# A tuned attention-and-FFN kernel: loads moved to the head of each round's queue, stores and read-backs behind them, rounding moved into the FFN's first steps

## The chip, the core and the metric

The kernel runs on one core of a Trainium2 chip. The metric is the device time of one execution in microseconds. Before the change three runs took 468.0, 469.41 and 469.4 us; the median is 469.4 us. The profiled execution is a fourth run.

## The reference

The input x has 4 sequences of 512 tokens with 512 features, in float32. The block is an attention-like mixer and then a feed-forward network (FFN), each with a layer norm ahead and a residual around it:

```python
q  = fft(heads(layernorm(x) @ W_q.T))       # 16 heads of 32
kv = fft(heads(layernorm(x) @ W_kv.T))
q, kv = q / norm(q), kv / norm(kv)          # over each head's spectrum
v = ifft(q * cumsum(kv, over tokens)).real
x = x + v @ W_o.T
gate = silu((layernorm(x) @ fp8(gate_w)) * gate_scale)   # 512 -> 1536
up   = (layernorm(x) @ fp8(up_w)) * up_scale
x = x + ((gate * up) @ fp8(down_w)) * down_scale         # 1536 -> 512
```

`fp8(w)` rounds a float32 weight to the nearest float8_e4m3fn value and keeps it as float32. The kernel does this rounding itself.

## The kernel before, in words

**Set-up.** The Fourier matrix is folded into W_q and W_kv, and its inverse into W_o, so that a spectrum is one matrix product. The layer norm's division is left to a per-token factor.

**Rounds.** The tokens are cut into 16 chunks of 128 (N = 16; four chunks to a sequence). One round handles one chunk i, but its steps are spread over several rounds. The program is scheduled by hand: the order of the calls is the order of the instructions on each engine, and the engines wait for each other's semaphores. In round i:

- PE computes the key spectrum of chunk i (`spectrum(i, 1)`, line 368, pq<-wkv), a small transpose (line 356), the query spectrum (`spectrum(i, 0)`, pq<-wq), the running sum of chunk i-1 (line 423, cum<-kh and kl) and the output projection of chunk i-3 (line 467, po).
- DVE scales keys and queries of chunk i-1 (line 392, kn and qn), adds the projection to x (`finish(i - 4)`, line 475), subtracts the rounded part of kn (line 414, kl), transposes the read-back of chunk i-3 (`v_turn`, line 330, qvT<-zv), sums squares (line 384), centres xT of chunk i+1 (`x_center`, line 360) and forms the products of chunk i-1 (lines 440 and 441).
- ACT squares (line 379), rounds kn to kh (line 409), takes the mean of x of chunk i+2 (`x_mean`, line 291) and the deviation of chunk i+1 (line 299).
- POOL computes inverse square roots (lines 301 for the deviations, 389 for the norms rn) and combines the products into qv (`combined`, lines 449 and 450).
- SP's queue issues the transfers in program order: the chunk's two loads for round i+2 (`load_xT`, line 105; `load_x`, line 110), the store of the attention's result (`finish`, line 476, y_all), the raw FFN weights (`load_unit`, line 206, rawf), and for the first sequence the load of ys from y_all (`load_y`, line 485). It also stores qv (`v_out`, line 453) and reads it back in blocks (`v_back`, line 325, four transfers, zv). A transfer that has to wait holds up all that stand behind it in the queue.

In rounds 9 to 12 the statistics of ys (`y_stats`) are computed for the first sequence's FFN; their last step, dev_f, is one POOL instruction (line 301).

**Rounding of the FFN weights.** The weights are cut into 18 units of 128 x 1024. A unit goes through a list of parts on DVE: for a gate or up unit add, (first step of the next unit), sub (lines 248, 229 or 233, 256); for a down unit floor, add, (first step), sub (lines 243, 250, 229 or 233, 258). The list has 60 parts. `next_parts(n)` takes the next n of them; after an add it puts the next unit's absolute value on ACT (`quant_abs`: one instruction at line 218 for a down unit, three at lines 221 to 223 for the others), and outside the rounds a down unit's first step also puts one instruction on POOL (line 239; in the rounds it is ACT's, line 237). Parts use two sets of work buffers, so the absolute value of unit u waits for the sub of unit u-2. The array `given` says how many parts a round takes; a round's parts stand at three places in it.

**FFN.** For each of 4 sequences there are 12 steps (n = 0 to 47 in all). A step is 16 products into gate and up (`inner`, line 539, gu), Silu on ACT (line 550, g), the product with up on DVE (line 552, f), rounding (ACT line 556, fh) and the rest (DVE line 558, fl); then 8 products with the down weights for the step before (`down`, line 573, pd). gate and up have one accumulation bank each, so g of a step must be done before PE starts the next step's gate products, and f before its up products. Parts are taken between f and fl (`between`) and behind the step (`behind`); in step 0 only behind. The last chunks' projections and stores lie in steps 0 to 4, as hooks `on_pe` and `behind`.

**Buffers.** Seven buffers of 8 KB per partition (pool `big`) hold the raw and folded weights, raw FFN units (two units share one), ys, yh and yl.

Of the kernel before, what the change touches and what calls it, by code (L numbers as in the profile page):

```python
# [35 lines left out]
def tile_fft_attention_then_fp8_ffn(  # L36
# [44 lines left out]
    TC = S // P  # L81
# [1 line left out]

    ctx.enter_context(tc.manual_schedule())
    const = ctx.enter_context(tc.tile_pool(name="const", bufs=1))
    big = ctx.enter_context(tc.tile_pool(name="big", bufs=7))
    work = ctx.enter_context(tc.tile_pool(name="work", bufs=2))
    ps = ctx.enter_context(tc.tile_pool(name="ps", bufs=2, space=PSUM))
    dram = ctx.enter_context(tc.tile_pool(name="dram", bufs=1, space=bass.MemoryType.DRAM))
# [4 lines left out]
    N = len(chunks)  # L94
# [18 lines left out]
    def big_tile(name, dtype=F32):  # L113
        return big.tile([P, KC, D], dtype, tag="big", name=name)
# [68 lines left out]
    U1 = 12  # L183
# [14 lines left out]
    def load_unit(u):  # L198

        _, src, n, k = units[u]  # L200
        staged[u] = big_tile("rawf") if k == 0 else staged[u - 1]
        if src is down_w:
            rows = src[n * KC * P : (n + 1) * KC * P, :]
        else:
            rows = src[:, n * D : (n + 1) * D]
        nc.sync.dma_start(
            staged[u][:, k : k + QH, :],
            rows.rearrange("(k p) n -> p k n", p=P)[:, k : k + QH, :],
        )

    def quant_abs(u):
        _, src, _, k = units[u]
        w = staged[u][:, k : k + QH, :]
        a = work.tile([P, QH, D], F32, tag="qa", name=f"qa_{u}")
        m = work.tile([P, QH, D], F32, tag="qm", name=f"qm_{u}")
        c = None
        if src is down_w:
            nc.scalar.activation(a, w, AF.Abs, scale=DOWN)
        else:
            c = work.tile([P, 1], F32, tag="qc", name=f"qc_{u}")  # L220
            nc.scalar.activation(a, w, AF.Abs, scale=UP)
            nc.scalar.activation(m, a, AF.Relu, scale=FAR, bias=far, accum_out=c)
            nc.scalar.activation(c, c, AF.Identity, scale=HUGE, bias=least)
        quant[u] = (w, a, m, c)
# [48 lines left out]
    def next_parts(n, in_rounds=False):  # L273

        for f, u in parts[:n]:
            if f is quant_step:
                f(u, in_rounds)
                if in_rounds and u + 2 < U1 and u != 1:
                    wanted.append(u + 2)
            else:  # L280
                f(u)
            if f is quant_add and u + 1 < len(units):
                quant_abs(u + 1)
        del parts[:n]
# [19 lines left out]
    def stats(src, name):  # L304
        less = mean(src, name)
        return less, deviation(src, less, name)
# [13 lines left out]
    def blocks(z, there):  # L320


        src = there.rearrange("(i t) (k j f) -> j t k i f", t=HD, j=P // HD, f=HD)
        for j in range(P // HD):
            nc.sync.dma_start(
                z[j * HD : (j + 1) * HD].rearrange("t k (i f) -> t k i f", f=HD), src[j]
            )

    def turned(t, z):
        nc.vector.transpose(t.rearrange("p k n -> p (k n)"), z.rearrange("p k n -> p (k n)"))  # L330
# [9 lines left out]
    def nm(i):  # L340
        return "%d_%d" % chunks[i]
# [20 lines left out]
    def spectrum(i, j):  # L362
        if j == 1:
            pqs[i] = {}
        pq = ps.tile([P, D], F32, tag="acc", name=f"pq{j}_{nm(i)}", bufs=4)
        w = (wq, wkv)[j]
        for k in range(KC):
            nc.tensor.matmul(  # L368
                pq, lhsT=xTs[i][:, k, :], rhs=w[:, k, :], start=k == 0, stop=k == KC - 1
            )  # L370
        pqs[i][j] = pq
# [9 lines left out]
    def summed(i, j):  # L381
        sq = sss[i, j]
        ss = work.tile([P, H], F32, tag=f"ss{j}", name=f"ss{j}_{nm(i)}")
        nc.vector.tensor_reduce(ss, heads(sq), AX.X, ALU.add)  # L384
        sss[i, j] = ss
# [15 lines left out]
    def k_scaled(i):  # L401
        kn = work.tile([P, D], F32, tag="kn", name=f"kn_{nm(i)}", bufs=1)
        scaled(i, 1, kn)
        if i in carries:
            row = carries.pop(i)
            nc.vector.tensor_tensor(kn[:1, :], kn[:1, :], row, ALU.add)
        kh = work.tile([P, D], F32R, tag="kh", name=f"kh_{nm(i)}", bufs=3)
        kl = work.tile([P, D], F32R, tag="kl", name=f"kl_{nm(i)}", bufs=3)
        nc.scalar.copy(kh, kn)
        kns[i] = (kn, kh, kl)  # L410
# [41 lines left out]
    def v_out(i):  # L452
        nc.sync.dma_start(qv_all[i], qvs.pop(i)[0])

    def v_back(i):
        zs[i] = work.tile([P, KC, P], F32, tag="z", name=f"zv_{nm(i)}")
        blocks(zs[i], qv_all[i])

    def v_turn(i):
        qvTs[i] = work.tile([P, KC, P], F32, tag="qvT", name=f"qvT_{nm(i)}", bufs=1)  # L460
        turned(qvTs[i], zs.pop(i))

    def project(i, tag="b"):
        po = ps.tile([P, D], F32, tag=tag, name=f"po_{nm(i)}")
        qvT = qvTs.pop(i)
        for k in range(KC):
            nc.tensor.matmul(  # L467
                po, lhsT=qvT[:, k, :], rhs=wo[:, k, :], start=k == 0, stop=k == KC - 1
            )
        pos[i] = po  # L470
# [10 lines left out]
    def load_y(b, chunks=None):  # L481
        if b not in ys:
            ys[b] = big_tile(f"ys_{b}")
        for c in range(TC) if chunks is None else chunks:
            nc.sync.dma_start(ys[b][:, c, :], y_all[b, c])

    def y_stats(b, c):
        st_y[b, c] = stats(ys[b][:, c, :], f"f{b}_{c}")
# [100 lines left out]
    def pair(n):  # L589

        return range(2 * n, 2 * n + 2) if 0 <= n < TC // 2 else ()

    def at(f, i, *more):
        if 0 <= i < N:
            f(i, *more)
# [83 lines left out]
    products(1)  # L679
    combined(1)  # L680
    v_back(0)
    v_out(1)
    summed(2, 0)
    norms(2, 0)
    next_parts(2, True)


    given = [2 if i in (6, 8, 10) else 3 for i in range(N - 3)] + [2, 2, 0]
    for i in range(3, N):
        spectrum(i, 1)  # L690
        at(load_xT, i + 2)
        k_scaled(i - 1)
        at(finish, i - 4)
        at(load_x, i + 2)
        while wanted:
            load_unit(wanted.pop(0))
        if 0 <= i - (N - 9) < TC:
            load_y(0, [i - (N - 9)])
        v_back(i - 2)
        k_low(i - 1)  # L700
        v_turn(i - 3)
        at(x_row, i + 1)
        squared(i, 1)
        at(x_deviation, i + 1)
        next_parts(given[i] // 3, True)
        q_scaled(i - 1)
        summed(i, 1)
        norms(i, 1)
        spectrum(i, 0)
        next_parts((given[i] + 1) // 3, True)  # L710
        running(i - 1)
        squared(i, 0)
        carry(i - 1)
        at(x_mean, i + 2)
        if 0 <= i - (N - 7) < TC:
            y_stats(0, i - (N - 7))
        at(x_center, i + 1)
        products(i - 1)
        combined(i - 1)
        v_out(i - 1)  # L720
        if i == N - 1:
            y_transpose(0, TC - 2)
            y_transpose(0, TC - 1)
        summed(i, 0)
        norms(i, 0)
        for c in pair(i - (N - 3)):
            y_norm(0, c)
        next_parts((given[i] + 2) // 3, True)
        project(i - 3)
        if i == N - 2:  # L730
            y_transpose(0, 0)
            y_transpose(0, 1)

    v_back(N - 2)
    load_unit(U1)
    load_unit(U1 + 1)
    load_y(1)
    finish(N - 4)  # L740
    k_scaled(N - 1)
# [4 lines left out]
    def on_pe(n, part):  # L746
        if part == 1 and n == 0:
            running(N - 1)
            products(N - 1)
            combined(N - 1)  # L750
            v_out(N - 1)
            project(N - 3, "tp")
            v_back(N - 1)

    def on_act(n):
# [3 lines left out]

    def between(n):  # L760
        if 0 < n < MC:
            next_parts(1)

    def behind(n):
        b, m = divmod(n, MC)
        if n == 1:
            load_unit(U1 + 2)
            load_unit(U1 + 3)
            finish(N - 3)
            v_turn(N - 2)  # L770
        elif n == 2:
            project(N - 2, "tp")
            v_turn(N - 1)
        elif n == 3:
            finish(N - 2)
            project(N - 1, "tp")
            load_unit(U1 + 4)
            load_unit(U1 + 5)
        elif n == 4:
            finish(N - 1)  # L780
        if b + 1 < B:
            if m == 0 and b > 0:
                load_y(b + 1)
            if 0 <= m - 7 < TC:
                y_turn(b + 1, m - 7)
            if 0 <= m - 4 < TC:
                y_norm(b + 1, m - 4)
                y_blocks(b + 1, m - 4)
        if b == 0:
            next_parts(2)  # L790
        if b + 1 < B and 0 <= m - 3 < TC:
            y_deviation(b + 1, m - 3)
# [77 lines left out]
```

## Time and profile before

| | us |
|---|---|
| median of the runs | 469.4 |
| profiled execution | 470.05 |
| its span, first to last instruction | 468.3 |
| set-up and rounds 0 to 2 (to the start of round 3) | 40.5 |
| rounds 3 to 15 (to the first FFN product) | 149.8 |
| FFN and the last stores | 278.0 |

The granted clock of TensorE was 0.997 of full speed. In the profile's timelines a row gives the start in us from the span's start, the duration, the engine, the line, the operation, what it writes and reads, and in brackets how long the engine had been idle and what ended that wait. SPq is SP's queue: its rows are the issues of transfers, not their data.

### The profile page before, as it was taken

The page shows a single profiled execution, that of the slowest core. Times are in us where ns is not written, and L with a number is a line of the kernel's source. Part 1 is how long each engine was busy: PE and PEld are TensorE (multiplying, and loading weights), DVE is VectorE, ACT ScalarE, POOL GpSimd, SP SyncE. Part 2 cuts the span into 40 slices and gives each one's busy share as a digit, 9 for nine tenths or more (in the row PEclk, how much of TensorE's full clock was granted, in tenths as well). Part 3 has the DMA queues.
Part 4 walks back from the last instruction along what each step waited for, and adds up shares of the span by engine and source line. Part 5 has one row for each costly group of instructions (what it writes and reads, how often), then busy time and mean ns, then how long its engine had stood idle before and what let it go on. Part 6 is the DMA issues. An engine that isn't in the chain of part 4 may idle for free.

```text
span 468.3 us, 5038 instructions
## 1 busy us (share of the span) xinstructions
PE 454.3 (97%) x1672; PEld 307.9 (66%) x1672; DVE 281.2 (60%) x387; ACT 213.2 (46%) x429; POOL 189.5 (40%) x133
## 2 busy tenths in 40 slices
PE   6999999999999989999999999999999999999995
PEld 6544344444444435676888888888888888888883
DVE  1549898998789789886797353333433332522325
ACT  3663664655576553255763225533236433222220
POOL 0248887899778677620043140112210022400002
PEclk9999999999999999999999999999999999999998
DMA  8733466657554632374442050340040430200002
GB/s 280 282 112 90 115 189 177 184 169 208 156 146 121 176 78 65 69 235 142 149 98 45 0 172 9 83 97 0 23 158 24 96 61 1 90 1 0 0 1 90
DMA packets 82586, 49.13 MB, mean 105 GB/s; under 512 B 62080, under 2 KB 62464, under 8 KB 82560
## 3 DMA queue, kind: packets, MB, share of 16 engines
q1 hardware_dynamic: 82176, 48.79, 36.9%
q8 instruction: 13, 0.21, 0.2%
q14 instruction: 13, 0.11, 0.1%
q10 hardware_dynamic: 384, 0.03, 0.1%
HBM read 33.04 MB, written 15.73 MB: 104 GB/s over the span
## 4 chain that ended last, share of the span: by engine, by line
PE 66%; POOL 14%; DVE 9%; issue 5%; ACT 4%; DMA 1%; SPq 0%; ACTq 0%; DVEq 0%; POOLq 0%
PE gu L539 37%; PE pd L573 19%; POOL rn L389 10%; PE po L467 4%; PE pq L368 3%; POOL qv L449 2%; POOL qv L450 1%; DVE ss L384 1%; PE pkv L164 1%; ACT sq L379 1%; DVE wu L256 1%; DVE qv L440 1%; PE pw L179 1%; DVE cross L441 1%; DVE kn L392 1%
## 5 line engine op out<-in xcount | busy, mean ns | idle before, releaser
L389 POOL TENSOR_TENSOR rn<-ss,nhalf 128x16 f32<-128x16 f32 x32 | 105.5, 3297 | 14.1 <-DVE ss L384 14.1
L552 DVE SCALAR_TENSOR_TENSOR f<-gu,gus,g 128x512 f32<-128x512 f32 x48 | 36.0, 750 | 110.8 <-PE gu L539 109.0
L539 PE MATMUL gu<-yh,wg 128*128 128x512 f32 x192 | 76.4, 398 | 0.0
L573 PE MATMUL pd<-wd,fl 128*128 128x512 f32 x192 | 74.8, 390 | 0.0
L573 PE MATMUL pd<-wd,fh 128*128 128x512 f32 x192 | 74.8, 389 | 0.0
L539 PE MATMUL gu<-yh,wu 128*128 128x512 f32 x192 | 74.8, 389 | 0.0
L539 PE MATMUL gu<-yl,wg 128*128 128x512 f32 x192 | 74.8, 389 | 0.0
L539 PE MATMUL gu<-yl,wu 128*128 128x512 f32 x192 | 74.7, 389 | 0.0
L556 ACT CAST fh<-f 128x512 fp32r<-128x512 f32 x48 | 29.8, 621 | 80.6 <-DVE f L552 80.6
L368 PE MATMUL pq<-wkv,xT 128*128 128x512 f32 x128 | 58.3, 598 | 2.4 <-DVE xT L360 2.4
L550 ACT ACTIVATE g<-gu,gus 128x512 f32<-128x512 f32 x48 | 33.0, 687 | 59.9 <-PE gu L539 59.6
L467 PE MATMUL po<-wo,qvT 128*128 128x512 f32 x128 | 57.9, 595 | 0.4
L368 PE MATMUL pq<-wq,xT 128*128 128x512 f32 x128 | 57.6, 593 | 0.0
L558 DVE TENSOR_TENSOR fl<-f,fh 128x512 fp32r<-128x512 f32 x48 | 35.8, 745 | 27.6 <-ACT fh L556 27.5
L585 POOL TENSOR_TENSOR o<-o,ys 128x512 f32<-128x512 f32 x14 | 17.7, 1290 | 81.7 <-DVE o L583 72.7
L368 PEld LDWEIGHTS pq<-wkv,xT 128*128 128x128 f32 x128 | 23.7, 190 | 33.4 <-issue 25.3
L301 POOL TENSOR_TENSOR dev_f<-dev_f,nhalf 128x1 f32<-128x1 f32 x16 | 10.1, 629 | 88.0 <-ACT dev_f L300 86.3
L539 PEld LDWEIGHTS gu<-yl,wg 128*128 128x128 f32 x192 | 36.1, 188 | 8.3 <-issue 1.0
L368 PEld LDWEIGHTS pq<-wq,xT 128*128 128x128 f32 x128 | 23.2, 190 | 27.8 <-issue 26.9
L539 PEld LDWEIGHTS gu<-yh,wg 128*128 128x128 f32 x192 | 36.0, 188 | 8.3 <-issue 0.5
L573 PEld LDWEIGHTS pd<-wd,fl 128*128 128x128 f32 x192 | 36.1, 188 | 7.6 <-DVE fl L558 0.2
L539 PEld LDWEIGHTS gu<-yh,wu 128*128 128x128 f32 x192 | 36.0, 188 | 7.5
(89 smaller groups left out, 607.3 us busy)
## 6 DMA issues: line engine op xcount, KB each, us to landing
x<-in_x SPq DMA_DIRECT2D x16, 256.0 KB, 4.1
xT<-in_xT SPq DMA_DIRECT2D x16, 256.0 KB, 2.9
qv_all<-qv SPq DMA_DIRECT2D x16, 256.0 KB, 2.0
zv<-qv_all SPq DMA_DIRECT2D x64, 64.0 KB, 4.1
y_all<-x SPq DMA_DIRECT2D x16, 256.0 KB, 3.0
ys<-y_all SPq DMA_DIRECT2D x16, 256.0 KB, 4.2
out<-o SPq DMA_DIRECT2D x16, 256.0 KB, 2.1
rawf<-in_gate_w SPq DMA_DIRECT2D x6, 512.0 KB, 5.0
```

The source lines that it names most:

```text
L301: nc.gpsimd.tensor_tensor(rstd, rstd, nhalf[:, 0:1], ALU.pow)
L368: nc.tensor.matmul(pq, lhsT=xTs[i][:, k, :], rhs=w[:, k, :], start=k == 0, stop=k == KC - 1)
L389: nc.gpsimd.tensor_tensor(rns[i, j], sss.pop((i, j)), nhalf, ALU.pow)
L449: on.tensor_tensor(vh[:, :, 1:HK], vh[:, :, 1:HK], vh[:, :, HK + 1 :], ALU.subtract)
L467: nc.tensor.matmul(po, lhsT=qvT[:, k, :], rhs=wo[:, k, :], start=k == 0, stop=k == KC - 1)
L539: nc.tensor.matmul(p, lhsT=w[:, k, m * P : (m + 1) * P], rhs=v[:, k, :], start=k == 0 and v is yhs[b], stop=k == KC - 1 and v is yls[b],)
L550: nc.scalar.activation(g, pgu[0], AF.Silu, scale=gus[:, 0, m : m + 1])
L552: nc.vector.scalar_tensor_tensor(f, pgu[1], gus[:, 1, m : m + 1], g, ALU.mult, ALU.mult)
L556: nc.scalar.copy(fh, f)
L558: nc.vector.tensor_tensor(fl, f, fh.bitcast(F32), ALU.subtract)
L573: nc.tensor.matmul(pds[b][c], lhsT=v[:, c * P : (c + 1) * P], rhs=wd[:, m, :], start=m == 0 and v is fused[n][0], stop=m == MC - 1 and v i ...
L585: add.tensor_tensor(o, o, ys[b][:, c, :], ALU.add)
```

## The change

- The pool `big` has eight buffers, not seven.
- In each round, the two loads for round i+2 and the load of ys go to the head of the queue, ahead of the stores and raw loads.
- `v_out` of a chunk is no longer called at the end of its round but one round later, right ahead of its own `v_back`, behind the loads, the y_all store and the raw loads.
- `y_stats` moves from ahead of `x_center`, `products` and `combined` to behind them.
- `given` is lowered: rounds 11 and 12 take two parts, not three; round 13 one, not two; round 14 none, not two. Steps 1 to 3 of the FFN take three parts, not one, between f and fl.
- At the end of the rounds and in the first FFN steps, raw units 12 and 13 are loaded ahead of the store and read-back of chunk 14, units 14 and 15 ahead of the read-back of chunk 15, and units 16 and 17 in step 1 (before: step 3).

The sum of the work is the same, but for one instruction: in the FFN the first step of unit 10 puts its extra instruction on POOL, where the round's version puts it on ACT. In the built program SP's load of units 14 and 15 waits for DVE and ACT (the last use of units 8 and 9), and that of units 16 and 17 for the last use of units 10 and 11.

```diff
-    big = ctx.enter_context(tc.tile_pool(name="big", bufs=7))
+    big = ctx.enter_context(tc.tile_pool(name="big", bufs=8))
...
     v_back(0)
-    v_out(1)
     summed(2, 0)
...
-    given = [2 if i in (6, 8, 10) else 3 for i in range(N - 3)] + [2, 2, 0]
+    given = [2 if i in (6, 8, 10, 11, 12) else 3 for i in range(N - 3)] + [1, 0, 0]
     for i in range(3, N):
+
+        at(load_xT, i + 2)
+        at(load_x, i + 2)
+        if 0 <= i - (N - 9) < TC:
+            load_y(0, [i - (N - 9)])
         spectrum(i, 1)
-        at(load_xT, i + 2)
         k_scaled(i - 1)
         at(finish, i - 4)
-        at(load_x, i + 2)
         while wanted:
             load_unit(wanted.pop(0))
-        if 0 <= i - (N - 9) < TC:
-            load_y(0, [i - (N - 9)])
+        v_out(i - 2)
         v_back(i - 2)
...
         at(x_mean, i + 2)
-        if 0 <= i - (N - 7) < TC:
-            y_stats(0, i - (N - 7))
         at(x_center, i + 1)
         products(i - 1)
         combined(i - 1)
-        v_out(i - 1)
+        if 0 <= i - (N - 7) < TC:
+            y_stats(0, i - (N - 7))
...
-    v_back(N - 2)
     load_unit(U1)
     load_unit(U1 + 1)
+    v_out(N - 2)
+    v_back(N - 2)
     load_y(1)
...
             v_out(N - 1)
             project(N - 3, "tp")
+            load_unit(U1 + 2)
+            load_unit(U1 + 3)
             v_back(N - 1)
...
         if 0 < n < MC:
-            next_parts(1)
+            next_parts(3 if n < 4 else 1)
...
         if n == 1:
-            load_unit(U1 + 2)
-            load_unit(U1 + 3)
             finish(N - 3)
             v_turn(N - 2)
+            load_unit(U1 + 4)
+            load_unit(U1 + 5)
...
             project(N - 1, "tp")
-            load_unit(U1 + 4)
-            load_unit(U1 + 5)
```

## The prediction

> **What bounds the kernel now.** I read the engine rows of the page first, then the timeline of PE, then those of SP, ACT and POOL around the places where PE starts late.
>
> ```profile
> PE 454.3 (97%) x1672; PEld 307.9 (66%) x1672; DVE 281.2 (60%) x387; ACT 213.2 (46%) x429; POOL 189.5 (40%) x133
> ```
>
> PE is busy for 97% of the span, so only its lost time can be won. Busy time has modelled ends; I therefore count from start to start. Each round i begins with the key spectrum, pq<-wkv. Cut at these starts, rounds 10 to 14 look so (length of the stretch, then the busy time of each engine):
>
> ```profile
> core 0: us, PE busy (x) PEld busy (x) DVE busy (x) ACT busy (x) POOL busy (x), PEclk, DMA share, GB/s
> 118.20:129.10 10.90, 10.90 (x29) 4.81 (x27) 7.73 (x12) 5.27 (x13) 8.00 (x6) 1.00 0.53 166
> 129.10:141.36 12.26, 11.67 (x28) 4.83 (x27) 9.94 (x15) 8.80 (x21) 9.60 (x7) 1.00 0.58 136
> 141.36:152.70 11.34, 11.14 (x28) 4.92 (x28) 10.34 (x15) 7.97 (x19) 9.52 (x7) 1.00 0.45 133
> 152.70:164.31 11.61, 11.15 (x28) 4.92 (x28) 8.49 (x12) 6.62 (x16) 7.94 (x7) 1.00 0.69 172
> 164.31:178.37 14.06, 12.65 (x35) 5.84 (x36) 12.20 (x18) 7.35 (x15) 10.97 (x6) 1.00 0.34 71
> ```
>
> Rounds 6 to 10 start 10.88 to 10.90 us apart, with no idle PE: that is PE's own floor. Rounds 11, 12, 13 are 1.38 + 0.46 + 0.73 longer; in PE's timeline the next spectrum then waits for DVE's centred xT. Round 14 holds eight transposes (0.87), so it loses 2.31; in it the running sum waits 1.06 for kh. Together 4.9 us. Round 15 and the FFN run without a gap (a step is 5.44 us again and again), and round 3, 12.34 us long, loses 1.46. DVE, ACT and POOL keep their order up to round 8, so that one stays. Why rounds 11 to 13 are long is seen in three queues at once.
>
> ```profile
> 135.30 0.33 SPq L453 DMA_DIRECT2D qv_all<-qv  x1
> 135.73 0.38 SPq L105 DMA_DIRECT2D xT<-in_xT  x1
> 136.20 0.40 SPq L476 DMA_DIRECT2D y_all<-x  x1
> 136.65 0.43 SPq L110 DMA_DIRECT2D x<-in_x  x1
> ...
> 146.64 0.33 SPq L453 DMA_DIRECT2D qv_all<-qv  x1
> ```
>
> ```profile
> 141.23 0.63 ACT L291 ACTIVATE each<-x 128x512 f32<-128x512 f32 x1 [2.47 <-DMA x<-in_x]
> ...
> 143.92 0.29 ACT L300 ACTIVATE dev_f<-dev_f,eps 128x1 f32<-128x1 f32 x1
> ```
>
> ```profile
> 144.29 0.55 POOL L301 TENSOR_TENSOR dev_f<-dev_f,nhalf 128x1 f32<-128x1 f32 x1 [0.81 <-ACT dev_f L300]
> 144.81 0.70 POOL L449 TENSOR_TENSOR qv<-qv 128x240 f32<-128x240 f32 x1
> 145.59 1.02 POOL L450 TENSOR_TENSOR qv<-cross 128x240 f32<-128x240 f32 x1
> ```
>
> This is a ring. The store of qv stands ahead of the loads, so x is issued 1.35 us after it and lands 4.58 later; ACT waited 2.47 for it and then needs 2.9 to reach dev_f; POOL takes dev_f ahead of qv; the next qv store follows at 146.64. The ring takes 11.34 us, and 11.75 the next time (146.64 to 158.39): more than PE's 10.88. The lag that it leaves is what makes kh late in round 14.
>
> **Part 1: loads first, store and read-back behind.** xT and x of round i+2 now follow the previous round's read-back, which waits for nothing of this round. The ring is cut: x no longer waits for qv. The cost is at the store. y_all (waits for DVE's x) and, in eight rounds (4, 5, 6, 8, 9, 10, 12, 13), a 512 KB raw load now stand ahead of the qv store, and the read-back stands right behind it and waits for its landing. When the store led the queue it landed in 2.0 us (the page's median). The row that is nearest to the new order is at the end of the rounds:
>
> ```profile
> 196.84 1.08 SPq L206 DMA_DIRECT2D rawf<-in_gate_w  x2
> 198.01 1.95 SPq L485 DMA_DIRECT2D ys<-y_all  x4
> 200.06 0.38 SPq L476 DMA_DIRECT2D y_all<-x  x1
> 200.54 0.40 SPq L453 DMA_DIRECT2D qv_all<-qv  x1
> 207.23 2.60 SPq L325 DMA_DIRECT2D zv<-qv_all  x4
> ```
>
> Here the store stood behind 2.36 MB and its read-back was issued 6.7 us later: 2.6 MB in 10.4 us, 0.25 MB per us. The Trainium skill (DMA: Bandwidth & Descriptors, "Queues, rings and completion order") speaks against the change: the engines consume a queue's descriptors in ring order, and a transfer's semaphore lands only after the earlier writes of that engine. By the 2.0 us row the wait is unchanged; by the rule, at this row's rate, 1.05 MB (y_all, raw, qv) need 4.2 us plus some 2 to land, less 0.95 already gone: 5.2 us. I take 5. Then zv is complete about 0.1 + 0.45 (y_all's issue) + 0.5 (raw's) + 5 + 2.6 (the read-back's four issues) + 2.7 (landing of the last; 2.2 at least, 4.1 in the median) = 11.4 us after DVE's x. In round 4 x ends at 58.03, so zv is there at 69.4, where the turn began at 68.54: DVE waits 0.9. The centred xT would be done at 73.8 instead of 72.9; PE needs it at 74.68. In round 8, with a ys load too, x ends at 100.39, zv comes at some 112.5 where the turn began at 110.19; xT is then done near 117.6, and PE needs it at 118.20. So the cost is nothing, covered by 0.6 us at the tightest place; each us that landing takes beyond that is lost in that round. If landing stays at 2.0, nothing is lost either.
>
> x itself: the read-back ends at most 2.8 us into the next round, xT, x and landing make it 8.2; ACT takes it 8.8 after the round's start at the earliest (round 8: 105.21 - 96.44). Covered; what is late next is zv.
>
> **Part 2: ys statistics behind the combining.** On POOL four dev_f (0.55 each) move behind qv; qv no longer waits for ACT (0.8 to 2.5 us a round). The next norms wait at most for dev_f, which is then done. Nothing is added.
>
> **Part 3: five rounding parts leave rounds 11 to 14 (one, one, one, two).** A part takes DVE 0.6 to 1.2 us from start to start; most are 1.2. DVE was busy 9.94, 10.34, 8.49 and 12.20 us in these rounds; without five parts (some 5.3 us) and with the ring cut, the heaviest has about 10 of its 11.75. POOL is busy 8 to 11 us with its 3.3 us norms, so it has no more than one us of room in a round. I let 0.7 us of the 4.9 stay: **4.2 us won**.
>
> **Part 4: these parts in the FFN.** DVE takes them between f and fl and behind the step. Steps 1, 2, 3 hold five parts instead of three. In the built program's order on DVE, with start-to-start costs f 0.67, fl 0.60, x and turn 0.6 each, L256 1.20, L243 1.14, L250 1.11, L258 1.13, L248 1.16, L229 and L233 0.60, in the times of before:
> - Step 1: f at 201.78, three parts 3.45, fl from 205.9 to 206.5; PE wants it at 206.97. Then x, turn, two parts: the next f starts at 209.5 instead of 207.25.
> - Step 2: its third part waits for ACT's three-instruction abs chain (2.57 us); fl ends at 214.3, wanted at 215.85. The turn of the last chunk comes at 214.3 instead of 212.41, and is wanted at 217.67. L258 ends at 216.1.
> - Step 3: here ACT counts. The abs chain of unit 13 needs the buffer that this L258 frees, and stands ahead of g on ACT: 216.1 + 2.57, so g runs from 218.7 instead of 214.24; PE needs its bank at 221.1. Unit 14's chain starts at 222.05, ahead of y's deviation (1.04) and the next g, which ends at 226.35; PE needs it at 226.56.
> - Step 5: g ends at 232.0, needed at 232.0. From unit 16 on the chain is one instruction of 1.06, and ACT catches up.
>
> No wait appears if every row keeps its mean; but margins are 0.0 to 0.5 at three places. DVE parts beside POOL's L239 took up to 1.73 (199.39), 0.5 more. POOL has one such operation more, since unit 10's moves from ACT (1.15). I charge **0.6 us**; bounds 0 and 2.
>
> **Part 5: the eighth buffer.** Raw units 8 and 9 now live beyond round 14, where yh and yl need two buffers; that is what it pays for. Loads of units 14, 15 come some 9 us earlier, at 201, ahead of the last read-back: 1.2 us of issue and 1 MB behind the store. That read-back waited to 207.23 before, so it is not later. Loads 16, 17 wait for the last use of units 10, 11 (about 212) and two y_all stores stand behind them on SP; those y rows are read one batch later. Cost nothing; bounds -0.3 and 0.3.
>
> **The sum.** 468.3 - 4.2 + 0.6 = 464.7 us of span. The profiled execution took 470.05, 1.75 around its span, so 466.45 of its own time; the median of the runs, 469.4, is 0.65 below it: **465.8 us**.
>
> **Rivals.**
> - All of the 4.9 comes back and the FFN holds: 464.5. For it: rounds 6 to 10 ran at the floor with up to three parts.
> - The read-back takes the ring's place: landing behind the raw load takes 6.5, not 5, and rounds 7, 9 and two later ones lose 0.5 each: 467.6. For it: 6.7 was seen. Against: with 2.36 MB ahead, not 0.8.
> - The rounds stay bound by POOL's norms and DVE, and the cut ring was only the last of equal waits; 0.7 comes back: 468.9, no change. Against: DVE waits of 2.18 us for POOL begin with dev_f's wait.
> - Slower: in FFN steps 1 to 3 the parts run at 1.7 instead of 1.2 beside POOL: fifteen parts, 7.5 us later, less 1.2 of margin: 6.3 lost through ACT's g behind the abs chain, 469.4 - 4.9 + 6.3 = 470.8 or more. It decides from L258 of step 2 ending after 218. Against: one part of twenty here took as long.
>
> **Chances.** The forecast 0.55, all back 0.13, read-back 0.14, no change 0.10, slower 0.08. About 0.3% (1.4 us) is what a measurement of this kernel can tell from no change. Faster below 468.0: 0.80, with part of the read-back case left to the same, 0.12; slower 0.08. The range reaches from all back with run scatter (463.6) to the no-change case (469.3).
>
> **What would show it.** Right: rounds 11 to 13 start 10.9 apart and round 14 takes 11.8; no ACT wait on x; dev_f behind qv; qv to zv 4 to 6 us in rounds with a raw load; in steps 3 to 5 PE gaps under 0.5 us before gu. Wrong: turns that wait for zv with PE waiting for xT or qvT behind them; gaps before gu or pd of over 1 us in steps 1 to 5; rounds 11 to 13 above 11.3 without an x wait.

## The result and the profile after

The changed kernel takes 465.0 us (median of four runs, 464.31 to 465.4) where the kernel before took 468.9 beside it: a ratio of 0.9917, 95% interval 0.9894 to 0.9941. The profiled execution took 465.4 us, its span 463.6. The prediction said 465.8 for the median and 464.7 for the span.

This is the row of engines on the page of the changed kernel, and then its time cut at the starts of rounds 11 to 15 (columns as in the table by round before):

```profile
PE 452.5 (98%) x1672; PEld 308.5 (67%) x1672; DVE 280.9 (61%) x387; ACT 211.9 (46%) x428; POOL 192.6 (42%) x134
```

```profile
core 0: us, PE busy (x) PEld busy (x) DVE busy (x) ACT busy (x) POOL busy (x), PEclk, DMA share, GB/s
...
129.38:140.25 10.87, 10.87 (x28) 4.99 (x27) 9.41 (x14) 8.79 (x20) 9.86 (x8) 1.00 0.57 143
140.25:151.14 10.89, 10.89 (x29) 5.00 (x28) 9.43 (x14) 8.72 (x21) 9.87 (x6) 1.00 0.58 158
151.14:162.01 10.87, 10.87 (x28) 4.99 (x27) 7.32 (x13) 4.97 (x13) 8.75 (x7) 1.00 0.62 168
162.01:173.77 11.76, 11.76 (x37) 5.82 (x35) 10.00 (x15) 3.80 (x8) 10.26 (x8) 1.00 0.33 77
```

PE is busy without a gap in all four stretches, as in the two rounds before them. Rounds 11, 12 and 13 went from 12.26, 11.34 and 11.61 us to 10.87, 10.89 and 10.87; round 14 went from 14.06 to 11.76, which is the floor and its eight transposes. All of the 4.9 us came back. From the start of round 10 to the FFN's first product (its row starts at 189.86 before and at 185.01 after) it is 71.66 us before and 66.51 after: 5.15 us, since round 15 is 0.25 shorter as well. The FFN and the last stores take 278.39 us before and 278.60 after; the start-up was 0.30 longer in this execution. 5.15 - 0.21 - 0.30 = 4.64, the difference of the two spans before rounding (468.26 and 463.61). (By these starts the last two rows of the table of before are 149.4 and 278.4, not 149.8 and 278.0.)

The medians differ by less, 3.9, because the profiled execution of before was 1.2 above the median of its runs and that of the changed kernel 0.4. There is one trace of before, and its excess lies most likely in the rounds: its round 10 starts at 118.20 (117.6 to 119.0 in the ten other traces that differ only later), and its FFN takes as long as in the other traces with the same FFN (278.4). A median execution of before would then have a stretch of 468.7 - 1.75 - 118.3 - 278.4 = 70.3 us; this is an estimate, from the 1.75 us that the profiled execution took beyond its span and the mean start of these ten. The 5.15 is thus about 3.8 in a median execution. In the later comparisons the executions of before spread from 467.3 to 471.2, those of the changed kernel by 1.1. Of the 15 above 470, nine show a mean granted clock of 0.995 or less, of the other 53 two; where in them the clock fell is not known.

SP's queue in round 10 and after it: the loads stand ahead, and the store of qv stands behind y_all and the raw load.

```profile
120.48 0.43 SPq L110 DMA_DIRECT2D x<-in_x  x1
...
121.48 0.38 SPq L476 DMA_DIRECT2D y_all<-x  x1
121.90 0.43 SPq L206 DMA_DIRECT2D rawf<-in_up_w  x1
122.43 0.43 SPq L453 DMA_DIRECT2D qv_all<-qv  x1
128.22 2.61 SPq L325 DMA_DIRECT2D zv<-qv_all  x4
...
131.59 0.38 SPq L110 DMA_DIRECT2D x<-in_x  x1
132.81 0.33 SPq L476 DMA_DIRECT2D y_all<-x  x1
133.23 0.38 SPq L453 DMA_DIRECT2D qv_all<-qv  x1
136.36 2.61 SPq L325 DMA_DIRECT2D zv<-qv_all  x4
```

The read-back waits for the store's landing: 5.8 us with a raw load ahead of the store, 3.1 without. ACT gets x in time now; it waits for nothing but its own last transfer's issue:

```profile
138.45 0.63 ACT L291 ACTIVATE each<-x 128x512 f32<-128x512 f32 x1 [0.60 <-ACT end L430]
...
141.13 0.29 ACT L300 ACTIVATE dev_f<-dev_f,eps 128x1 f32<-128x1 f32 x1
```

And POOL takes dev_f behind qv; when qv starts (140.19), ACT has not yet computed dev_f (141.13 to 141.42):

```profile
140.19 1.40 POOL L449 TENSOR_TENSOR qv<-qv 128x240 f32<-128x240 f32 x1
141.68 0.70 POOL L450 TENSOR_TENSOR qv<-cross 128x240 f32<-128x240 f32 x1
142.33 1.00 POOL L301 TENSOR_TENSOR dev_f<-dev_f,nhalf 128x1 f32<-128x1 f32 x1
```

### The profile page after: what moved, and what is told of

It reads as the page before. It is cut to its first block, busy times and chain, and to the rows that moved or that the text cites. A ratio compares the mean times of both kernels' runs of the same rounds, so it can differ in the third digit from the quotient of the medians.

```text
span 463.6 us, 5026 instructions
## 1 busy us (share of the span) xinstructions
PE 452.5 (98%) x1672; PEld 308.5 (67%) x1672; DVE 280.9 (61%) x387; ACT 211.9 (46%) x428; POOL 192.6 (42%) x134
## 4 chain that ended last, share of the span: by engine, by line
PE 92%; DVE 3%; ACT 3%; issue 1%; DMA 1%; ACTq 0%; SPq 0%; DVEq 0%
PE gu L539 38%; PE pq L368 19%; PE pd L573 19%; PE po L467 11%; PE cum L423 1%; PE pkv L164 1%; PE pw L179 1%; ACT sq L379 1%; PE pw L164 1%; ACT qm L222 1%; DMA raw<-in_w_kv 1%; ACT each L299 0%; ACT qa L221 0%; PE pt_f L317 0%; DVE ss L384 0%
## 5 line engine op out<-in xcount | busy, mean ns | idle before, releaser
L389 POOL TENSOR_TENSOR rn<-ss,nhalf 128x16 f32<-128x16 f32 x32 | 103.6, 3238 | 16.3 <-DVE ss L384 13.8
L301 POOL TENSOR_TENSOR dev_f<-dev_f,nhalf 128x1 f32<-128x1 f32 x16 | 12.5, 781 | 72.1 <-ACT dev_f L300 72.0
```

The lines of the kernel that those rows point to most:

```text
L301: nc.gpsimd.tensor_tensor(rstd, rstd, nhalf[:, 0:1], ALU.pow)
L389: nc.gpsimd.tensor_tensor(rns[i, j], sss.pop((i, j)), nhalf, ALU.pow)
```

## The experiments

Three things are changed: the queue order (Q), the place of the ys statistics (Y), and the moved parts with the eighth buffer and the earlier raw loads (P). Runs 1 to 6 are all the other combinations of the three. The traces are compared by one number, the stretch from the start of round 10 to the FFN's first product, which leaves out the start-up; the medians and ratios are of runs beside the kernel before (median 468.7 in each of the three groups; 468.9 beside the change itself). The stretch is that of one execution. The one of before was 1.4 above the median of 468.7 and that of run 1 1.3 above its own, all others of the table within 0.5, so differences of the stretch against these two can be off by that much; the medians stand beside them.

| run | kernel | median us | ratio to before, 95% | stretch us | rounds 10 to 14 us |
|---|---|---|---|---|---|
| | before | 468.7 | | 71.66 | 10.90 12.26 11.34 11.61 14.06 |
| 1 | Q | 468.05 | 0.9979 (0.9966 to 0.9993) | 70.13 | 11.40 11.21 11.21 10.98 13.83 |
| 2 | Y | 466.13 | 0.9927 (0.9900 to 0.9953) | 67.55 | 10.89 10.87 10.88 10.88 12.54 |
| 3 | P | 466.88 | 0.9951 (0.9927 to 0.9975) | 68.69 | 10.88 10.96 12.19 10.98 12.43 |
| 4 | Q, Y | 466.26 | 0.9934 (0.9908 to 0.9959) | 67.55 | 10.88 10.88 10.88 10.88 12.54 |
| 5 | Y, P | 465.12 | 0.9921 (0.9900 to 0.9943) | 66.51 | 10.88 10.88 10.88 10.88 11.75 |
| 6 | Q, P | 465.39 | 0.9931 (0.9912 to 0.9951) | 66.90 | 10.88 10.88 10.88 10.88 12.14 |
| | Q, Y, P: the change | 465.0 | 0.9917 (0.9894 to 0.9941) | 66.51 | 10.88 10.87 10.89 10.87 11.76 |

**Run 1, the queue order alone.**

```diff
     for i in range(3, N):
+        at(load_xT, i + 2)
+        at(load_x, i + 2)
+        if 0 <= i - (N - 9) < TC:
+            load_y(0, [i - (N - 9)])
         spectrum(i, 1)
...
+        v_out(i - 2)
         v_back(i - 2)
...
         combined(i - 1)
-        v_out(i - 1)
```

> The kernel before with only the queue order of the change (loads first, store of qv behind y_all and raw load); ys statistics ahead of the combining, rounding parts and buffers as before. Ring theory: the ring is cut at SP, rounds 11 to 13 start 10.9 apart, round 14 (two parts in it) loses up to 1; span some 464.9, median 465.5 to 466 (3 less than before). Rival (the parts on DVE and the POOL work of these rounds are what is late): nothing in them changes, rounds 11 to 14 still lose over 3.5, median 468 to 469.

It won 1.5 us of the stretch and 0.6 of the median: far from the 3 of the ring theory, and inside the rival's range, but not nothing. ACT's waits for x are gone, and yet rounds 11 and 12 take 11.21. POOL shows both reasons: first the wait for the first dev_f (round 9's statistics), then a turn in which it waits only for DVE's sums of squares.

```profile
121.83 0.66 POOL L301 TENSOR_TENSOR dev_f<-dev_f,nhalf 128x1 f32<-128x1 f32 x1 [2.30 <-ACT dev_f L300]
...
139.81 3.89 POOL L389 TENSOR_TENSOR rn<-ss,nhalf 128x16 f32<-128x16 f32 x1 [0.94 <-DVE ss L384]
143.66 1.25 POOL L301 TENSOR_TENSOR dev_f<-dev_f,nhalf 128x1 f32<-128x1 f32 x1
144.89 0.70 POOL L449 TENSOR_TENSOR qv<-qv 128x240 f32<-128x240 f32 x1
145.66 1.03 POOL L450 TENSOR_TENSOR qv<-cross 128x240 f32<-128x240 f32 x1
146.66 2.90 POOL L389 TENSOR_TENSOR rn<-ss,nhalf 128x16 f32<-128x16 f32 x1
...
151.01 3.88 POOL L389 TENSOR_TENSOR rn<-ss,nhalf 128x16 f32<-128x16 f32 x1 [0.93 <-DVE ss L384]
```

```profile
149.59 0.75 DVE L392 SCALAR_TENSOR_TENSOR qn<-pq,dev,rn 128x512 f32<-128x512 f32 x1 [0.89 <-POOL rn L389]
150.26 0.67 DVE L384 TENSOR_REDUCE ss<-sq 128x16 f32<-128x512 f32 x1
```

The second is a loop of two engines: POOL's key norm, dev_f, qv, query norm, then DVE's qn and ss, then POOL's next key norm: 139.81 to 151.01, 11.20 us, with no wait but the hand-overs. Cutting the ring at SP leaves this loop, and dev_f in it. The other runs show which of the two counts.

**Run 2, the ys statistics alone.** The kernel before, with this edit only:

```diff
-        if 0 <= i - (N - 7) < TC:
-            y_stats(0, i - (N - 7))
         at(x_center, i + 1)
         products(i - 1)
         combined(i - 1)
         v_out(i - 1)
+        if 0 <= i - (N - 7) < TC:
+            y_stats(0, i - (N - 7))
```

> The kernel before with only the ys statistics moved behind the combining. Ring theory: the ring is cut at POOL, since qv no longer waits for ACT, but ACT still gets x late; half or more of the 4.9 comes back, span some 465.8, median 466.5. Rival (SP's order or the parts count, dev_f's place does not): median 468 to 469.

This one edit wins 4.1 of the stretch's 5.15 us and 2.5 of the median: rounds 11 to 13 are at the floor, with SP's queue and all parts as before. The POOL rows of the same place as the first of run 1:

```profile
113.76 3.88 POOL L389 TENSOR_TENSOR rn<-ss,nhalf 128x16 f32<-128x16 f32 x1 [0.38 <-DVE ss L384]
117.61 0.70 POOL L449 TENSOR_TENSOR qv<-qv 128x240 f32<-128x240 f32 x1
...
120.09 0.56 POOL L301 TENSOR_TENSOR dev_f<-dev_f,nhalf 128x1 f32<-128x1 f32 x1 [0.56 <-ACT dev_f L300]
```

qv follows its norm at once. dev_f comes at the same time as before (120.08 there): ACT is not earlier, it only no longer holds up qv. The row of before, for comparison:

```profile
120.08 0.55 POOL L301 TENSOR_TENSOR dev_f<-dev_f,nhalf 128x1 f32<-128x1 f32 x1 [2.48 <-ACT dev_f L300]
```

The ring is cut at POOL just as well, because qv no longer waits for anything that x feeds: in rounds 10 to 12 ACT's longest wait for x is 1.04, where it was 3.73. The loop of POOL and DVE is not cut: dev_f stays in it, one place later, and it takes 11.35 us here (key norm at 136.72, the next at 148.07), no less than in run 1. DVE's turns (qn to qn) are 11.48, 11.49 and 11.35, all above 10.88, and PE loses nothing in rounds 10 to 13. So what this edit takes away is the one wait of round 9, and not the loop.

**Run 3, the moved parts alone.** `given`, the FFN's parts, the eighth buffer and the raw loads as in the change; queue and statistics as before.

```diff
-    given = [2 if i in (6, 8, 10) else 3 for i in range(N - 3)] + [2, 2, 0]
+    given = [2 if i in (6, 8, 10, 11, 12) else 3 for i in range(N - 3)] + [1, 0, 0]
...
-            next_parts(1)
+            next_parts(3 if n < 4 else 1)
```

> The kernel before with only the five rounding parts moved into the FFN's first steps, the eighth buffer and the earlier raw loads. Ring theory: the ring stays, rounds 11 to 13 still take 11.3 to 11.7, only round 14 gains; span some 466.5, median 467. Rival (parts are the load that is late): rounds 11 to 13 go to 10.9, all comes back, median 465 or less.

As the ring theory had it in the median (466.88), but not in the shape: the ring did not hold each round at 11.3 to 11.7. DVE's turn from one qn to the next, from round 9 on 13.61, 12.26, 11.34 and 12.20 us before, is 13.10, 12.01, 11.59 and 10.73 here: the lag of round 9 stays, and comes out at PE in round 12 (1.04 of waiting for xT).

**Run 4, the parts undone.** Queue order and statistics, everything else as before.

```diff
-    given = [2 if i in (6, 8, 10, 11, 12) else 3 for i in range(N - 3)] + [1, 0, 0]
+    given = [2 if i in (6, 8, 10) else 3 for i in range(N - 3)] + [2, 2, 0]
...
-            next_parts(3 if n < 4 else 1)
+            next_parts(1)
```

> The changed kernel without the moved parts and the eighth buffer: queue order and ys statistics alone. Ring theory: rounds 11 to 13 start 10.9 apart with their three, three and two parts; round 14 with two parts loses up to 1 through kh; the FFN's 0.2 comes back; median 465 to 466. Rival (parts needed): rounds 11 to 14 lose 2 or more, median 467 or more.

466.26 us, between the two. The stretch is that of run 2 to 0.01 us: on top of the statistics the queue order is worth nothing. The parts are worth 67.55 - 66.51 = 1.04 on top of both: 0.78 in round 14 and 0.25 in round 15. From here the theory was another: what counted is that qv waited for dev_f, and not SP's order.

**Run 5, the queue order undone.** The changed kernel with the loads and `v_out` back in the places of before.

```diff
-        at(load_xT, i + 2)
-        at(load_x, i + 2)
         spectrum(i, 1)
+        at(load_xT, i + 2)
         k_scaled(i - 1)
         at(finish, i - 4)
+        at(load_x, i + 2)
...
-        v_out(i - 2)
         v_back(i - 2)
...
         combined(i - 1)
+        v_out(i - 1)
```

> The changed kernel with its queue order undone (the order of the kernel before: qv store first, loads behind it); ys statistics behind the combining, moved parts and eighth buffer stay. New theory after the first four runs (what counted was that qv on POOL waited for dev_f; SP's order is not on the path): rounds 10 to 13 at 10.88, round 14 at 11.8, median 464.8 to 465.2, as the whole change. The prediction's ring (x late behind the qv store holds ACT and by it the round): ACT waits on x again, rounds 11 to 13 lose 0.3 to 0.7 each, median 466 or more.

465.12 us, where the new theory had it, and the same stretch as the change. ACT does not wait for x at all in rounds 9 to 13, although the loads stand behind the qv store again. The largest part of the diff makes no difference that these runs can tell.

**Run 6, the statistics undone.** The changed kernel with `y_stats` back ahead of `x_center`.

```diff
+        if 0 <= i - (N - 7) < TC:
+            y_stats(0, i - (N - 7))
         at(x_center, i + 1)
         products(i - 1)
         combined(i - 1)
-        if 0 <= i - (N - 7) < TC:
-            y_stats(0, i - (N - 7))
```

> The changed kernel with only the ys statistics put back ahead of the combining; queue order, parts and buffer stay. New theory: in round 9 POOL's qv waits 2.3 to 2.7 for the first dev_f, dev_f stays in the loop of POOL and DVE, whose turn with fewer parts is 10.9 to 11.2; some 1.5 is lost in rounds 10 to 14, median 466 to 466.5. The prediction's ring (cut at SP already): nothing is lost, median 465.

465.39 us, nearer to the prediction's ring than to the new theory. The wait came as foreseen, and DVE's turn took 13.11 there:

```profile
119.97 0.67 POOL L301 TENSOR_TENSOR dev_f<-dev_f,nhalf 128x1 f32<-128x1 f32 x1 [2.45 <-ACT dev_f L300]
```

But the next turns, with fewer parts, took 11.21, 10.61 and 10.74, so the lag shrank again before PE met it, and only 0.39 of the expected 1.5 was lost (in round 14). Queue order and parts without the statistics thus win 4.76 of the 5.15 us, more than the statistics alone. The wait costs PE time only where the later turns keep its lag.

**Run 7, the FFN's extra parts crowded into step 1.**

```diff
         if 0 < n < MC:
-            next_parts(3 if n < 4 else 1)
+            next_parts(6 if n == 1 else 2 if n == 2 else 1)
```

> The changed kernel with the FFN's extra parts crowded: six parts between f and fl in step 1, two in step 2, one in step 3 (instead of three, three, three). Cover theory of part 4 (fl of step 1 has 0.5 us of room): three more parts of 1.1 to 1.2 make fl 3 us late, PE waits 2.5 to 3.3 for it before the down products, median 467.5 to 468.3. Rival (PE finds other work, or the down products come later): under 0.5, median 465.5 or less.

470.21 us, ratio 1.0028 (1.0013 to 1.0042): 5.1 to 5.2 slower than the change, more than the expected 3.3. PE's rows, and then the windows around them:

```profile
202.32 0.39 PE L573 MATMUL pd<-wd,fh 128*128 128x512 f32 x1
206.03 0.50 PE L573 MATMUL pd<-wd,fl 128*128 128x512 f32 x1 [3.32 <-DVE fl L558]
...
208.09 4.93 PE L467 MATMUL po<-wo,qvT 128*128 128x512 f32 x8
```

```profile
core 0: us, PE busy (x) PEld busy (x) DVE busy (x) ACT busy (x) POOL busy (x), PEclk, DMA share, GB/s
...
207.00:208.00 1.00, 1.00 (x4) 0.82 (x4) 1.00 (x2) 0.00 (x0) 0.00 (x0) 0.67 0.55 209
208.00:209.00 1.00, 1.00 (x3) 0.40 (x2) 1.00 (x3) 0.00 (x0) 0.00 (x0) 0.50 0.15 53
209.00:210.00 1.00, 1.00 (x3) 0.48 (x2) 1.00 (x2) 0.40 (x1) 0.00 (x0) 0.50 0.48 57
210.00:211.00 1.00, 1.00 (x2) 0.38 (x2) 1.00 (x2) 0.49 (x2) 0.00 (x0) 0.62 1.06 408
```

fl was late by what the cover theory said, so its 0.5 us of room is real. The rest is the clock: after 3.32 us of idle PE the granted clock falls to 0.50, from 207.3 until about 210.8. The windows' losses, 0.33 + 0.50 + 0.50 + 0.38, are 1.7 us; 3.3 + 1.7 = 5.0. The Trainium skill has this rule (TensorE: Matmul & The Clock Gate, "Why this matters for your kernels": no idle gaps of PE above some 3 us between bursts of products, or the clock falls to half). The expectation had left it out: by the wait alone 468.3, with it 470; 470.21 was measured.

**Run 8, round 3 relieved.** No parts ahead of round 3; three instead of two in rounds 11 and 12.

```diff
     norms(2, 0)
-    next_parts(2, True)
...
-    given = [2 if i in (6, 8, 10, 11, 12) else 3 for i in range(N - 3)] + [1, 0, 0]
+    given = [2 if i in (6, 8, 10) else 3 for i in range(N - 3)] + [1, 0, 0]
```

> The changed kernel without the two rounding parts ahead of round 3, and with three parts instead of two in rounds 11 and 12 (the same parts in the same order, each up to two places later until there). If round 3's 1.47 comes from these parts on DVE ahead of the centred xT: round 3 takes 10.9 to 11.3, median 463.6 to 464. If it comes from DVE's and POOL's own chain at the start: round 3 stays 12.3, and rounds 12 to 14 may lose up to 1 through the parts: 465 to 466.

464.37 us, ratio 0.9909 (0.9890 to 0.9929), a little above the expected 464. Round 3's loss does come from the parts: it takes 11.13 instead of 12.35. These are DVE's rows at its start in the changed kernel, and then in run 8:

```profile
43.43 0.68 DVE L229 TENSOR_SCALAR qm<-qa 128x1024 int32<-128x1024 int32 x1
44.03 1.73 DVE L256 SCALAR_TENSOR_TENSOR wg<-qm,qc,qa 128x1024 fp32r<-128x1024 f32 x1
45.68 0.74 DVE L392 SCALAR_TENSOR_TENSOR kn<-pq,dev,rn 128x512 f32<-128x512 f32 x1
```

```profile
43.64 0.75 DVE L392 SCALAR_TENSOR_TENSOR kn<-pq,dev,rn 128x512 f32<-128x512 f32 x1 [0.46 <-POOL rn L389]
```

Counted from the round's start (40.78 and 40.45), kn came 1.7 us earlier. In round 7, though, another order of parts now falls due, and it takes 11.23; round 8 takes 10.99. Of 1.22 won 0.46 was given back there.

**Runs 9 and 10, which of the four statistics counts.** Both are run 1 (queue order alone) with part of run 2: in run 9 only the first of the four is behind the combining, in run 10 only the other three.

```diff
-        if 0 <= i - (N - 7) < TC:
+        if 0 < i - (N - 7) < TC:
             y_stats(0, i - (N - 7))
         at(x_center, i + 1)
         products(i - 1)
         combined(i - 1)
+        if i == N - 7:
+            y_stats(0, 0)
```

> The kernel of the first run (queue order alone) with only the first of the four ys statistics (round 9) behind the combining; the other three stay ahead of it. Theory of the one wait (ACT cannot give the first dev_f before some 120 us, so qv on POOL waits 2.3 there and the lag is never made up): nearly all of the gain of all four comes back, round 9's turn at qn takes 11.2 to 11.5 instead of 12.94, rounds 10 to 13 at 10.9, median 466 to 466.8. Theory of the loop (dev_f, 1.25 in every turn of POOL and DVE): 467.5 to 468.

> The kernel of the first run (queue order alone) with the first of the four ys statistics (round 9) ahead of the combining and the other three behind it. Theory of the one wait: the lag of 2.3 comes in round 9 as before and stays, median 467.6 to 468.1 as with none moved. Theory of the loop: rounds 10 to 13 go to 10.9 and the lag shrinks, median 466 to 466.8.

Run 9: 466.59 us, ratio 0.9950 (0.9931 to 0.9969), stretch 68.09. Run 10: 467.63 us, ratio 0.9973 (0.9959 to 0.9988), stretch 68.99. Between none moved (70.13) and all four moved (67.55), the first one is worth 2.04 and the other three together 1.14; the two overlap. By the medians, which don't rest on run 1's one traced execution, it is 1.5 and 0.4 of 1.8. Both fell where the theory of the one wait put them; in run 9 DVE's turn at the first dev_f is 11.22, in run 10 it is 13.12. The other three are not nothing: run 10 gained 0.4 of the median where none was expected.

**Run 11, a longer landing.** Two stores of 256 KB, of a constant to a place that nobody reads, ahead of the qv store.

```diff
+        if 4 <= i <= 13:
+            for k in range(2):
+                nc.sync.dma_start(spare[k], tab.rearrange("p a n -> p (a n)"))
         v_out(i - 2)
```

> The changed kernel with two more stores of 256 KB (a constant, to a place that nobody reads) ahead of the qv store in each of rounds 4 to 13, to lengthen the store's landing. Part 1 of the prediction (zv has 0.6 us of cover at the tightest place, all beyond it is lost): at 0.25 MB per us and 0.8 us of issue the read-back comes 2.5 to 3 us later; DVE waits 2 us and more for zv at the turn in rounds with a raw load, and 0.5 to 1.5 is lost in each of these: median 468 to 474. Rival (DVE's order has more room than that): zv is late, but nothing is lost, median 465 to 465.6.

471.27 us, ratio 1.0058 (1.0035 to 1.0081), so the cover can be used up; but not where it was expected. From qv's issue to its read-back's the time hardly grew (3.9 to 6.7 us, mean 5.1; 3.1 to 5.8, mean 4.7, in the changed kernel's same rounds): the stores cost SP some 1.1 us of issue ahead of qv, and the lag moves on from round to round. So this run tests a late zv, not a long landing. DVE waits for zv seven times, 12.4 us in all, but the first 3.85 us, in three rounds, cost only the 0.67 by which round 9 is longer. Then the waits come on top of each other. These are DVE's and then PE's rows of run 11 (its program has one line more, so line 331 is line 330):

```profile
127.81 0.71 DVE L331 STREAM_TRANSPOSE qvT<-zv 128x512 f32<-128x512 f32 x1 [1.94 <-DMA zv<-qv_all]
...
141.53 0.71 DVE L331 STREAM_TRANSPOSE qvT<-zv 128x512 f32<-128x512 f32 x1 [3.75 <-DMA zv<-qv_all]
```

```profile
128.58 3.70 PE L468 MATMUL po<-wo,qvT 128*128 128x512 f32 x8 [1.08 <-DVE qvT L331]
...
142.30 5.40 PE L468 MATMUL po<-wo,qvT 128*128 128x512 f32 x8 [2.58 <-DVE qvT L331]
```

Rounds 9 to 11 take 11.55, 12.32 and 15.42 us, and all others what they take in the change: 0.67 + 1.44 + 4.54 = 6.65. What PE waits for in the last two is the transposed read-back itself, for the output projection, not xT. The last wait cost more than itself again: eight projections took 5.40 instead of 3.70, at a granted clock of 0.50 from 143.3 to 146.7. This is of the traced execution, at 472.33; five of the seven show a mean clock of 0.997 or more, which leaves no room for such a drop.

**Run 12, a version that beats both.** Run 8 with one part moved from round 7 to round 13.

```diff
-    given = [2 if i in (6, 8, 10) else 3 for i in range(N - 3)] + [1, 0, 0]
+    given = [2 if i in (6, 7, 8, 10) else 3 for i in range(N - 3)] + [2, 0, 0]
```

> The kernel of the eighth run (no parts ahead of round 3) with one rounding part fewer in round 7 and one more in round 13. If the 0.35 and 0.11 lost in rounds 7 and 8 of that run come from the third part: both back at 10.88, median 463.8 to 464.1, provided that round 13 has room for a second part (round 14 at 11.75). If round 13 has no room: round 14 takes 12.2 or more, median 464.4 to 465.

463.49 us (463.25 to 463.63), ratio 0.9879 (0.9859 to 0.9899), 0.3 better than expected. Rounds 7 and 8 are at 10.88 again; round 14 takes 11.92, 0.16 more than in the change.

The eighth buffer and the earlier raw loads were changed only together with the parts. A version of the moved parts with seven buffers was not tried: yh or yl would have to wait for a buffer that comes free only after the FFN has started.

## Why the prediction was right, and where it was not

- **The bound** (PE's lost time, 4.9 us in rounds 11 to 14) was right: PE has no gap left there, and nothing else got shorter but round 15, by 0.25, which the sum did not have.
- **The cause** (the ring of store, load, ACT, POOL) was half of it, and that the number came near is in part luck. "The ring is cut: x no longer waits for qv" stands under part 1, and the cut at SP is worth 1.5 of 5.15 alone (run 1) and nothing beside the other two (runs 4, 5). The ring was in the trace: with the queue order alone ACT's waits for x are gone, and of POOL's waits for dev_f (2.48, 1.65, 0.81 and 1.55 before; the profile puts the last down to a transfer, but ACT's dev_f ends right ahead of it, at 156.29) only the first remains. But it was read back from rounds 11 to 13, where the time was lost, and the lag came from round 9: POOL stood 2.48 us at 117.6 to 120.08, before ACT could have any dev_f (119.71 to 120.00), and ACT had not waited for x there. That row was in the trace of before (it stands under run 2); the prediction listed the wait only as "0.8 to 2.5 us a round". The right outcome came from three edits that overlap: without the queue order all of the gain comes (run 5), without the statistics 4.76 of 5.15 (run 6), without the parts 4.1 (run 4). The signs listed under "What would show it" came true, but they don't tell the queue order from the rest: rounds 11 to 13 at 10.9 and, from round 9 on, no ACT wait on x are there in run 5 too.
- **Part 1** (costs nothing): right. The landing was taken at 5 us with a raw load ahead, by the Trainium skill's rule of ring order (DMA: Bandwidth & Descriptors, "Queues, rings and completion order"); from issue to issue it measured 4.1 to 5.8, which agrees, and 3.1 and 4.0 without a raw load (2.0 to 2.3 in rounds 3, 14 and 15). The working had DVE wait 0.9 for zv at the turn of 68.54 and 2.3 at that of 110.19. In the changed kernel it did not wait at the first and waited 0.62 at the second, and 0.38 one round later:

```profile
111.22 0.71 DVE L330 STREAM_TRANSPOSE qvT<-zv 128x512 f32<-128x512 f32 x1 [0.62 <-DMA zv<-qv_all]
```

  xT of that round is done at 116.08 and PE takes it at 118.50, so 2.4 us of cover were left, not 0.6. "Each us that landing takes beyond that is lost in that round" came out near in round 9 of run 11: the turn starts 3.0 later in its round than in the change, 0.6 beyond this cover, and 0.67 is lost. In the two rounds behind it the loss is larger and takes a path that the working did not have: the projection waits for qvT (1.08 and 2.58). The rounds carry lag on.
- **Part 2** (nothing is added): right in what it costs, and undervalued: this is the edit that wins 4.1 alone (2.5 of the median). The working saw that "qv no longer waits for ACT" and gave it no share.
- **Part 3** (five parts out of rounds 11 to 14, 0.7 of 4.9 stays): the size was off; 0.0 stays. Beside the other two edits it is worth 1.04, 0.78 of it in round 14; alone 2.97 (1.8 of the median).
- **Part 4** (0.6 lost in the FFN): 0.21 measured, in these two traces; over all traces but those of runs 7 and 11 0.15 (278.38 to 278.42 without the moved parts, 278.54 to 278.60 with them). The working held in the rows of g. The changed kernel's FFN starts 4.85 earlier; with the predicted times shifted by that, g of step 3 was predicted at 213.85 and starts at 213.99 behind the chain that waits for L258; g of step 4 was predicted to end at 221.50 and ends at 221.54; step 5's at 227.15, and ends at 227.16:

```profile
211.42 1.06 ACT L221 ACTIVATE qa<-rawf 128x1024 f32<-128x1024 f32 x1 [2.76 <-DVE wd L258]
213.99 0.67 ACT L550 ACTIVATE g<-gu,gus 128x512 f32<-128x512 f32 x1
...
226.49 0.67 ACT L550 ACTIVATE g<-gu,gus 128x512 f32<-128x512 f32 x1
```

  PE lost 0.09 and 0.15 at the starts of steps 6 and 7. The 0.6 was a margin for slower rows, and none came that PE felt.
- **Part 5** (cost nothing): no wait of PE in these steps.
- **The sum.** 468.3 - 4.2 + 0.6 = 464.7 against 463.6: 0.95 more came back, the FFN lost 0.39 less than the 0.6, and the start-up took 0.30 more. The span fell by 4.64 where 3.6 was forecast; the median fell by only 3.9 because the traced execution of before that the sum starts from was above its median.
- **The rivals.** All back was nearest in time (464.5). The read-back in the ring's place did not happen at 5.8 us, and does happen with the extra stores of run 11. The bound of POOL and DVE (no change): in run 1 their loop turned at 11.20 with no wait for x; but in run 2 it turned at 11.35 and PE lost nothing, so it does not bind by itself. The slower case (ACT's g behind the abs chain) has its mechanism in the rows above, at a loss of 0.2. Two of the rivals' sums are off: four losses of 0.5 on 465.8 make 467.8, not 467.6, and 0.7 won with 0.6 lost makes 469.3, as "Chances" has it, not 468.9.

## What to carry to other kernels

In a queue that an engine works off in order, look for an instruction that waits long ahead of one that others wait for, and price its first occurrence by itself: a lag of 2 us that comes once can be lost several rounds later, where the trace blames something else. When several edits work on one lag, their gains don't add: alone they won 1.5, 4.1 and 3.0 us here, together 5.15. Which edit could have been left out only the combinations show. Price a stall of PE of some 2.5 us and more with the slower clock that may follow it.

## What the runs showed of the hardware

- PE waits of 1.04 to 1.08 us left the granted clock at 1.00. After 2.58 us (run 11) and 3.32 us (run 7) it was 0.50, from 1.0 and 1.3 us after the end of the wait, for 3.4 us in both. The Trainium skill (TensorE: Matmul & The Clock Gate, "Why this matters for your kernels") puts the limit at some 3 us; in the trace of run 11 2.58 was enough. 3.4 us at half clock take the mean of an execution to 0.996 or less (an estimate: 0.5 x 3.4 / 470): in run 7 all fourteen executions are there, in run 11 only two of seven. How long PE waited in the other five is not recorded.
- A store of 256 KB was read back 2.0 to 2.3 us after its issue with nothing close ahead in the queue, 3.1 and 4.0 us behind a 256 KB store, and 4.1 to 5.8 us behind a 256 KB store and a 512 KB load.
- POOL's rows vary without a change of their work: the norm of 128 x 16 took 2.9 to 4.15 us, the same qv instruction (L449) 0.70 to 1.41, in rounds of the changed kernel. What runs beside them differs; no run here takes that apart.
